# Two attention layers on one core: first f and g made in place, small PSUM reads by ScalarE, last sums by query rows

## The chip, the cores and the metric

The kernel runs on one core of one Trainium2 chip. The metric is device time in microseconds (us), the median of several executions; in each comparison the kernel before ran on the same chip in the same rounds (runs 5 to 7 on another chip than the other runs). TensorE is the matrix engine, VectorE, ScalarE and GpSimd the element-wise ones (DVE, ACT and POOL in the profile), SyncE (SP) issues most DMAs. PSUM is the memory that TensorE writes its results to; the other engines read them from there.

## The reference, cut to what matters

Eight images of 64 channels by 4096 positions pass two self-attention layers. Layer 0 has 8-channel f and g and a residual; layer 1 normalises its input by groups first.

```python
# layer 0
f, g, hh = Wf x + bf, Wg x + bg, Wh x + bh        # 8, 8 and 64 channels
beta = softmax(f^T g, axis=keys);  x = x + hh beta^T
# layer 1
xn = group_norm(x, 8 groups);  q, k, v = split(w_qkv xn + b_qkv)
x = w_proj (softmax(q k^T / 8) v) + b_proj + x
```

No maximum is subtracted ahead of the exponentials; the kernel sums them plainly and checks at the end that every sum lies in a safe range, else a general path runs.

## The kernel before

Work is cut into chunks of 1024 queries (two halves of 512) and steps of 256 keys; 16 steps make a chunk, four chunks an attention. A step is: scores on TensorE, exponentials on ScalarE into a tile `e` (six buffers), `e` against the values on TensorE, and `e` added to the running sum on VectorE. The order is layer 0 of image 0, layer 0 of image 1, then layer 1 of image 0, layer 0 of image 2, and so on. Preparing the next attention is put between the steps of the running one as "units" at given steps. Names used below: `mu` is the mean of a channel group, `v` what its deviation is made from, `a` the factor of the normalisation and `xn` the normalised input. In its parts that matter:

```python
def project(self, k):                       # Layer 0: f and g of half the columns
    ...                                     # four matmuls into one PSUM pair
    nc.scalar.activation(full, ps, AF.Identity, bias=fgb)
    nc.vector.tensor_copy(high, full)       # high: bufs=1
    nc.vector.scalar_tensor_tensor(split, high.bitcast(F32), lowmask, full, ...)
    for ...:                                # 16 small DMAs into the row tiles f, g
        self.sent = nc.sync.dma_start(dst[rows, cols], split[...])

def means():                                # Layer 1, at step 21
    ps = pair()                             # one of three PSUM pairs
    matmul(ps[:, 0, 0:1], gavg, mv[:, 0:1], start=True, stop=True)
    nc.vector.tensor_copy(mu, ps[:, 0, 0:1])
    nc.vector.tensor_sub(d, mv[:, 0:1], mu)
    nc.vector.scalar_tensor_tensor(v, d, d, mv[:, 1:2], ...)

def deviations():                           # step 24
    matmul(ps[:, 0, 0:1], gavg, v, start=True, stop=True)
    nc.vector.tensor_scalar_add(ve, ps[:, 0, 0:1], EPS)
    ...                                     # 15 VectorE operations of 128x1: a = gamma / sqrt(ve)

def normal(c):                              # step 27 for c = 0
    nc.vector.tensor_scalar(xns[c], x, mu, self.a, ...)          # xn, 128x512
                                            # step 30: TensorE projects q and k from xn

def weigh(i, j, e, cols, now):              # once a step
    ...
    added = nc.vector.tensor_add(esum, first if t == 1 else esum, e).ins   # 128x2048
```

`issue_after` puts what follows behind a named instruction of the same engine, without a wait.

## Time and profile before

| | before |
|---|---|
| time, median of 3 (range); of 4, with the result | 3088.91 us (3087.74 to 3089.83); 3088.35 |
| span of the profiled execution | 3086.4 us |
| TensorE busy | 3043.7 us |
| first dense add of VectorE | 36.10 us |
| means matmul, then copy of mu | 222.48, 231.96 us |
| xn of the first layer-1 block starts | 251.73 us |
| last exponential of the second layer-0 attention ends | 340.18 us |
| last exponential of all ends; to the end of the span | 3067.55 us; 18.9 us |

The last rows are marks along the one road.

The stretch table has the busy time of each engine within a stretch of the span, the number of its instructions, and the granted TensorE clock as a share of full speed. Of the kernel before, around the first layer-1 preparation:

```profile
core 0: us, PE busy (x) PEld busy (x) DVE busy (x) ACT busy (x) POOL busy (x), PEclk, DMA share, GB/s
...
220.00:270.00 50.00, 43.66 (x279) 15.96 (x277) 47.53 (x43) 33.73 (x29) 0.00 (x0) 0.93 0.03 6
```

TensorE misses 6.3 of these 50 us and the clock is 0.93 of full, while VectorE is busy for all but 2.5: the engine that decides this stretch is not the one with the 99%.

### The profile page before, as it was taken

Reading aid. Unit: us, or ns where it says so; the run is one execution under the profiler, and the core shown is the slowest. Engines: PE = TensorE matmul, PEld = TensorE weight load, DVE = VectorE, ACT = ScalarE, POOL = GpSimd, SP = SyncE. Lnnn points to the kernel's source line nnn. Section 1 sums busy time; section 2 is a strip of 40 time slices with the busy share of each in tenths; the row PEclk is TensorE's granted clock in tenths of the full one; section 3 lists DMA queues with packets and bytes.
Section 4 is the critical chain, followed back from the end, with each engine's and each line's share of the span. In section 5 each row is a group of like instructions: output and inputs, shape, how many; then the busy total and the mean of one; then the engine's idle time right before and its main releaser. Section 6 shows DMA issues by size and latency. Waiting matters only on the chain.

```text
span 3086.4 us, 59347 instructions
## 1 busy us (share of the span) xinstructions
PE 3043.7 (99%) x26071; PEld 1132.3 (37%) x26071; DVE 2538.6 (82%) x1616; ACT 2038.7 (66%) x1971; POOL 16.5 (1%) x41
## 2 busy tenths in 40 slices
PE   7999999999999999999999999999999999999998
PEld 2333334333343333333334333343334333334433
DVE  7999877899768997689877898779987699776676
ACT  6877655786557865578555785558855587555554
POOL 2000000000000000000000000000000000000000
PEclk9999999999999999999999999999999999999999
DMA  3000010100101001010011000100011000000000
GB/s 85 22 8 11 18 39 15 32 1 15 39 19 28 1 15 39 22 25 1 15 39 25 22 1 20 41 19 22 1 29 32 19 8 1 15 22 15 11 12 12
DMA packets 57722, 63.06 MB, mean 20 GB/s; under 512 B 30848, under 2 KB 30928, under 8 KB 57456
## 3 DMA queue, kind: packets, MB, share of 16 engines
q1 hardware_dynamic: 56336, 59.03, 7.7%
q8 instruction: 206, 3.38, 0.5%
q14 instruction: 60, 0.49, 0.1%
q0 software_dynamic: 800, 0.15, 0.0%
q10 hardware_dynamic: 320, 0.01, 0.0%
HBM read 25.06 MB, written 8.65 MB: 11 GB/s over the span
## 4 chain that ended last, share of the span: by engine, by line
PE 95%; DVE 3%; ACT 1%; issue 1%; SPq 1%; DMA 1%; ACTq 0%; DVEq 0%
PE banks L137 95%; DVE esum_l L656 2%; ACT e_l L730 0%; SPq L426 0%; ACT e_l L771 0%; DMA x<-in_x_dram 0%; DMA w<-in_WgT_dram 0%; DVE vt_l L298 0%; DVE high_l L416 0%; DVE esum_l L311 0%; SPq L145 0%; DVE r_l L355 0%; DMA fg_l<-high_l 0%; ACTq L169 0%; DVE high_l L413 0%
## 5 line engine op out<-in xcount | busy, mean ns | idle before, releaser
L656 DVE TENSOR_TENSOR esum_l<-esum_l,e_l 128x2048 f32<-128x2048 f32 x896 | 2052.3, 2291 | 455.9 <-ACT e_l L730 402.9
L730 ACT ACTIVATE e_l<-banks 128x1024 f32<-128x1024 f32 x1024 | 992.8, 1021 | 801.7 <-PE banks L137 768.8
L137 PE MATMUL banks<-e_l,v_l 64*64 64x512 f32 (+2 forms) x8772 | 1100.9, 588 | 0.0
L771 ACT ACTIVATE e_l<-banks 128x2048 f32<-128x2048 f32 (+3 forms) x763 | 955.8, 1317 | 204.2 <-PE banks L137 201.8
L137 PE MATMUL banks<-kq_l 64*64 64x512 f32 (+1 forms) x8448 | 1009.8, 586 | 6.3 <-DVE mu_l L476 6.3
L137 PE MATMUL banks<-e_l,vt_l 128*64 128x512 f32 (+1 forms) x4064 | 832.0, 550 | 0.0
L137 PEld LDWEIGHTS banks<-e_l,v_l 64*64 64x64 f32 (+1 forms) x8772 | 362.3, 133 | 574.1 <-issue 531.5
L137 PEld LDWEIGHTS banks<-kq_l 64*64 64x64 f32 (+1 forms) x8448 | 348.3, 134 | 580.2 <-issue 540.2
L137 PEld LDWEIGHTS banks<-e_l,vt_l 128*64 128x64 f32 x4064 | 267.5, 137 | 473.7 <-issue 453.7
L137 PE MATMUL banks<-fg_l 32*128 32x512 f32 x1792 | 211.0, 460 | 8.0 <-ACT e_l L771 4.4
L656 DVE TENSOR_TENSOR esum_l<-e_l,e_l 128x2048 f32<-128x2048 f32 x64 | 146.4, 2288 | 18.6 <-ACT e_l L730 9.9
L137 PEld LDWEIGHTS banks<-fg_l 32*128 32x128 f32 x1792 | 86.3, 183 | 188.5 <-ACT e_l L771 135.6
L311 DVE TENSOR_TENSOR esum_l<-esum_l 128x1024 f32<-128x1024 f32 x64 | 78.1, 1220 | 0.9
L562 DVE COPY raw_l<-banks 128x512 f32<-128x512 f32 x32 | 22.1, 691 | 31.3 <-PE banks L137 31.3
L137 PE MATMUL banks<-esum_l,ones 128*32 128x256 f32 (+1 forms) x508 | 41.3, 393 | 4.5 <-DVE esum_l L311 2.8
L360 DVE TENSOR_TENSOR raw_l<-raw_l,r_l 128x512 f32<-128x512 f32 x64 | 43.8, 684 | 0.0
L536 ACT ACTIVATE kq_l<-banks,qkb 128x512 f32<-128x512 f32 x64 | 40.6, 696 | 0.0
L137 PE MATMUL banks<-xn_l,wqk 64*64 64x512 f32 x256 | 33.4, 592 | 0.0
L137 PEld LDWEIGHTS banks<-wh,x 64*64 64x64 f32 x1024 | 22.8, 140 | 16.1 <-issue 13.9
L137 PE MATMUL banks<-x,wfg 64*64 64x512 f32 x128 | 19.2, 648 | 9.0 <-DVE low L179 9.0
L137 PEld LDWEIGHTS banks<-wvp,xn_l 64*64 64x64 f32 x1024 | 20.6, 134 | 16.9 <-issue 16.6
L445 ACT COPY raw_l<-banks 128x512 f32<-128x512 f32 x32 | 19.0, 594 | 10.9 <-PE banks L137 10.8
(88 smaller groups left out, 378.4 us busy)
## 6 DMA issues: line engine op xcount, KB each, us to landing
r_l<-recips SPq DMA_DIRECT2D x126, 128.0 KB, 2.9
fg_l<-high_l SPq DMA_DIRECT2D x224, 64.0 KB, 2.0
x<-in_x_dram SPq DMA_DIRECT2D x32, 256.0 KB, 4.8
kq_l<-kq_l SPq DMA_DIRECT2D x64, 128.0 KB, 2.3
out_dram<-raw_l SPq DMA_DIRECT2D x64, 128.0 KB, 2.3
zt_l<-zs_l SPq DMA_DIRECT2D x252, 1.0 KB, 1.7
kq_l<-high_l SPq DMA_DIRECT2D x32, 64.0 KB, 2.0
recips<-stash SPq DMA_DIRECT2D x63, 4.0 KB, 1.4
```

Of the source, the lines that this page charges most:

```text
L137: in_order(nc.tensor.matmul(*args, **kwargs))
L311: nc.vector.tensor_add(esum[:, 0], esum[:, 0], esum[:, 1])
L360: nc.vector.tensor_mul(raw, raw, r)
L445: nc.scalar.copy(raw, acc[0])
L536: nc.scalar.activation(self.parts[:, h, cols], ps[:, h, :], AF.Identity, bias=k1["qkb"][:, h : h + 1],)
L562: nc.vector.tensor_copy(raw, acc[0])
L656: added = nc.vector.tensor_add(esum, first if t == 1 else esum, e).ins
L730: nc.scalar.activation(e[:, p], both_ps[p], AF.Exp, scale=at.scale)
L771: nc.scalar.activation(e.rearrange("k p h n -> k (p h) n")[:, first_ : first_ + n_, :], banks[:, bank : bank + n_, :], AF.Exp, scale=at.scale,
```

## The change

Four intents. **Head**: f and g of the first 512 columns are made with weights laid out so that they come out in their row tiles, without DMA; the loads are reordered; the other projections and values are put between the first steps. **Constants** and **means**: small PSUM reads move from VectorE to ScalarE. **End**: the last sums are made by query rows (128x8), inverted there, and laid out over channels by a product of ones with a diagonal; the range check of all but the last sums comes earlier. Its core:

```diff
+    direct = const.tile([P, 2, P], F32, name="direct")      # weights repeated for 128 rows
...
+        def project_direct(self):
+            for i, dst in enumerate((self.f, self.g)):
+                matmul(ps[:, i, :], direct[:, i, :], x_tiles[self.b][:, 0:CW], ...)
+                nc.scalar.activation(full[:, i, :], ps[:, i, :], AF.Identity, bias=bias2[:, i : i + 1])
+                nc.vector.tensor_copy(high[:, i, :], full[:, i, :])
+                nc.vector.scalar_tensor_tensor(dst[:, 0:CW], high[:, i, :].bitcast(F32), ...)
...
+                    self.project_direct()
+                    self.project(0, (1,))                    # columns 512 to 1023, 8 DMAs
+                return [(-1, begin, True), (0, rest, True)] + [ ... values at -1, 1, 5, 8 ]
...
-                nc.vector.tensor_copy(mu, ps[:, 0, 0:1])
+                nc.scalar.copy(mu, ps[:, 0, 0:1])
...
-                nc.vector.tensor_scalar_add(ve, ps[:, 0, 0:1], EPS)
+                nc.scalar.copy(ve, ps[:, 0, 0:1])
+                nc.vector.tensor_scalar_add(ve, ve, EPS)
...
-                nc.vector.tensor_copy(wvt[:, h, :], t0[:C, 0, 0:C])     # and wvp, biases
+                nc.scalar.copy(wvt[:, h, :], t0[:C, 0, 0:C])
...
-            added = nc.vector.tensor_add(esum, first if t == 1 else esum, e).ins
+            with tc.issue_after(layers0[0].split.ins) if i == 0 and t == 1 else nullcontext():
+                added = nc.vector.tensor_add(esum, first if t == 1 else esum, e).ins
...
+        def end(self, acc, esum, e, t):
+            for part in (esum[:, 1], e[:, 0], e[:, 1]):
+                nc.vector.tensor_add(total, total, part)
+            for i, (h, k) in enumerate(parts):
+                matmul(z[:, i : i + 1], total[:, h, ts(k, P)], ones[:, 0:1], ...)
+            nc.vector.reciprocal(rt, z);  bounds(rt, 1)
+            ...                             # diag = ident * rt
+            matmul(bad_ps, ...)             # the flag
+            matmul(laid[ts(h, C), :], ones, diag[...], ...)
+            nc.vector.tensor_mul(raw, raw, laid)
```

## The prediction

> **What bounds the kernel now.** I read the page's busy shares and chain first, then the waits of TensorE, then the timeline at the three places where those waits lie.
>
> ```profile
> PE 3043.7 (99%) x26071; PEld 1132.3 (37%) x26071; DVE 2538.6 (82%) x1616; ACT 2038.7 (66%) x1971; POOL 16.5 (1%) x41
> ...
> PE 95%; DVE 3%; ACT 1%; issue 1%; SPq 1%; DMA 1%; ACTq 0%; DVEq 0%
> ```
>
> TensorE is busy 3043.7 of 3086.4 us. The change takes no large matmul away, so all that can be won is its idle time, 42.7 us, plus work done at a low clock. The list of what TensorE waited for says where that is:
>
> ```profile
> PE banks L137 <- DVE low L179: 9.0, 1, 9.0
> PE banks L137 <- DVE bad L797: 6.5, 2, 3.5
> PE banks L137 <- DVE mu_l L476: 6.3, 1, 6.3
> PE banks L137 <- ACT e_l L771: 4.4, 7, 1.9
> PE banks L137 <- DVE esum_l L311: 2.8, 1, 2.8
> PE banks L137 <- DMA fg_l<-high_l: 2.6, 2, 1.7
> ```
>
> Three places: the start (9.0, 2.6, most of the 4.4), one stall at the means of the first layer-1 block (6.3), the end (6.5 + 2.8 + 5.5 after the last matmul). The eight blocks between repeat without a wait over 1 us. The head, by the timeline:
>
> ```profile
> 8.72 0.20 DVE L174 COPY wfg<-w 128x64 f32<-128x64 f32 x1 [7.71 <-DMA w<-in_WgT_dram]
> 14.32 10.62 SPq L426 DMA_DIRECT2D fg_l<-high_l  x16
> 20.86 1.33 PE L137 MATMUL banks<-fg_l 32*128 32x512 f32 x5 [1.73 <-DMA fg_l<-high_l]
> ...
> 36.10 21.46 DVE L656 TENSOR_TENSOR esum_l<-esum_l,e_l 128x2048 f32<-128x2048 f32 x9
> ```
>
> Weights land at 8.7, the projected f and g leave by 16 small DMAs of 0.66 us each to issue, and scores run only from 20.9. At 36.1 a dense run of VectorE adds begins. Its length decides my prediction:
>
> ```profile
> 222.48 0.38 PE L137 MATMUL banks<-mv_l,gavg 128*128 128x1 f32 x2
> ...
> 231.96 0.16 DVE L476 COPY mu_l<-banks 128x1 f32<-128x1 f32 x1
> ...
> 232.17 0.79 PE L137 MATMUL banks<-kq_l 32*128 32x512 f32 x2 [6.34 <-DVE mu_l L476]
> 232.90 5.07 PE L137 MATMUL banks<-e_l,v_l 128*64 128x512 f32 x12
> ...
> 251.73 0.55 DVE L504 TENSOR_SCALAR xn_l<-x,mu_l,a_l 128x512 f32<-128x512 f32 x1
> ...
> 253.00 1.09 PE L137 MATMUL banks<-xn_l,wqk 64*64 64x512 f32 x8
> ```
>
> The means leave TensorE at 222.9, but VectorE copies them only at 231.96: it is about 9 us behind. Pairing each add with the exponential that it adds, in the trace, the add starts 1.4 us after the exponential's end at 36 us, 3.7 at 176, 8.6 at 221, and never catches up before 240. In the first two layer-0 blocks one step costs VectorE 2.39 us (2.29 and a gap of 0.1) and TensorE some 2.3, so VectorE is the slower engine from 36 to 240 us; six e buffers hide it. With the same pairing, the next write of an e buffer comes 10 us after the add that frees it at the start and only 0.5 us after it at 224. The tail:
>
> ```profile
> 3073.84 3.35 DVE L355 RECIPROCAL r_l<-banks 128x512 f32<-128x512 f32 x1
> ...
> 3078.94 1.11 SPq L570 DMA_DIRECT2D out_dram<-raw_l  x2
> ...
> 3080.71 0.14 DVE L805 CAST n_bad<-banks 1x1 int32<-1x1 f32 x1 [0.28 <-PE banks L137]
> ```
>
> **What the Trainium skill says.** "TensorE: Matmul & The Clock Gate", section on the 16 sub-arrays: VectorE and ScalarE queues are strict first-in first-out. The trace agrees: the 0.16 us copy waits 9 us behind four ready adds. Same page, "What's actually happening": after an idle window of about 3.4 us the clock halves until a busy window has passed. The trace agrees: after the 6.34 us stall twelve records took 5.07 us, and 2.37 a little later, so the stall costs some 2.7 us more. "DMA: Bandwidth & Descriptors", "Issuing engines are not separate DMA queues": transfers interleave on the same engines whoever issues them. The last 2 KB piece of the weights took 5.9 us to land while the 1 MB of x was in flight, the first 1.9; the order of issue therefore counts. "ScalarE: Activation LUTs", "What ACT_TABLE_LOAD costs": 1283 ns; here 1.28, at 8.87, behind the bias DMAs.
>
> **The change, part by part.**
>
> Head. Weights are issued first, so I put them at 3.5 us, and the first 512 columns of x at 5 (256 KB by the 2 us latency and some 170 GB/s that the first loads show). The two direct products use all 128 rows: two records of 0.85 us each at the low clock, 1.7 per product: f until 6.8, g until 8.5, and the half product for columns 512 on until 10.2. ScalarE 0.7 each, VectorE cast 0.4 and split 0.7 each (half of the 0.8 and 1.28 for 1024 wide): f and g are ready at about 11, no DMA. But the first group of scores needs a bank that the copy of the values frees, and that copy stands on VectorE behind the cast and split of the half product: ScalarE 10.3 to 11.4, cast to 12.2, split to 13.5, copy to 14.1. So scores start near 14, not 20.9: 7 us earlier for TensorE, of which the rest projection (1.7) and three groups of values (1.1 each) are put back between steps, but TensorE is not the bound here. For VectorE: the 8 DMAs of the half product take 13.5 + 5.3 to issue and 2 to land, 20.9; only then may the cast of the rest overwrite the one "high" buffer, and the diff holds the first add until the rest's split is done: 20.9 + 0.8 + 1.28 = 23.0. Three adds of 2.39 later, at 30.2, VectorE is where it was at 36.1: **5.9 us earlier**. After that it also loses two copies of wvt (0.34), wvp (0.2), two bias adds (0.3) and the mu copy (0.2): 1.0 us. **Sum 6.9.**
>
> Means by ScalarE. The bank is freed at once, so the 6.34 us stall and its 2.7 us of low clock go. But the next small matmul ("deviations", three steps or 6.8 us of TensorE work later) needs v, and two operations of v still stand in VectorE's queue 9.5 us back: TensorE waits there for about 3 us. Then projecting the normalised x (253.0) needs xn, which VectorE makes in the same queue; before, TensorE came only 0.7 us after it. So TensorE at that point cannot gain more than VectorE does: 6.9, plus the 0.7, plus some 0.5 of true VectorE idle between 225 and 252: **8.1 us for head and means together**. The stall is cut into pieces rather than removed. In the other seven blocks the means lie in a layer-1 stage where each step of 3.43 us leaves VectorE 1.14 free: nothing to win.
>
> Constants by ScalarE: the 0.5 us wait for wvt is inside the 8.1.
>
> Tail. The last full add (2.29) and the fold (1.22) become three adds of 1024, from 3066.5 to 3070.2. Then 16 records for the sums by query rows; one pair of such 128-row, one-column records took 0.38 us, so some 0.12 each: 3072.3. The reciprocal of 128x8 takes 0.2 in place of 3.35; bounds 0.7, two products for the diagonal 1.4, the two PSUM reads of the totals 1.4 (before, these lay ahead of the fold): 3076.2. The laying out by ones (0.9) lies under the totals. Multiply and residual 1.5: 3077.7, against 3078.9. The flag is no longer last (0.41 + 0.68 + 0.69 + 0.15 + the matmul and cast behind the residual go). The program's end follows each engine's last instruction by a fixed branch of some 4 us and about 1 us of closing; before, that counted from 3080.85, now from the second DMA issue on ScalarE at 3078.3: **2.6 to 3 us**.
>
> Sum: 8.1 + 2.9 = 11.0; 3088.9 - 11.0 = 3077.9.
>
> **The rivals.** (1) TensorE is not held by VectorE: it then keeps its own head gain (7 and some low-clock time, less what is put back, 4 to 8) and all of 6.3 + 2.7, and the tail: 17 to 20 us, 3069 to 3072. For it: DMA-free scores. Against it: the 0.5 us of buffer left at 224 and the unbroken adds. (2) The head is not shorter for VectorE: x lands late, or the half product's 8 DMAs and the one buffer hold the first add until 26; then only the stall's remainder and the tail count, 4 to 6 us: 3083 to 3085. (3) A wait takes the stall's place and is long enough for the clock to fall in a stage where TensorE bounds again after 253; costs 2.7 of the 11: 3081. A loss over 2% (62 us) would need a new stall in each of the eight blocks of 7 us; ScalarE has over 1 us free in every layer-1 step, so two 0.2 us copies do not make one.
>
> **Range and chances.** Centre 3077.8. One side is rival (1) in part, the other (2) or (3): 3071 to 3083. Two per cent is 62 us, more than all of TensorE's idle time, so faster 0.01, same 0.985, slower 0.005.
>
> **What would show it.** Right: in the chain, adds from about 23 us on without a gap until 240; the waits list without mu, but with one for v of 2 to 4 us and one for xn; the first dense add run 6 us earlier; the project matmul of 253.0 near 245; from there to the end of the last layer-1 step the same duration; the second output DMA near 3078 on the old clock and 5 us from there to the end. Wrong: no wait for v or xn and over 15 us gained (VectorE did not bind), a first add later than 25 us, or e exponentials waiting for adds in the blocks after 400 us.

## More of the kernel before

A scheduler in the compiler orders each engine's instructions when the kernel is built.

In the traces VectorE works through its list in the built order.

For the first layer-1 block the built VectorE list reads (running sums are "add t", t the step within the second chunk of image 1):

```
before:   add 3 | mu d v | add 4 5 6 | ve, guess | add 7 | ... | add 10 | a  xn | add 11
```

## The result, and the profile after

The changed kernel takes 3088.99 us (median of 4, 3087.75 to 3089.58), the kernel before 3088.35 in the same rounds. The ratio is 1.0001 with a 95% interval of 0.9984 to 1.0018: nothing gained. Ratios here and below are the mean time of one kernel's runs over that of the other's runs of the same rounds, so not quite the ratio of the medians. A repeat (run 11) gave 3089.46 against 3089.17.

What TensorE waited for, changed kernel (total us, times, longest):

```profile
PE banks L137 <- DMA x<-in_x_dram: 7.3, 1, 7.3
PE banks L137 <- DVE v_l L570: 4.5, 1, 4.5
...
PE banks L137 <- DVE xn_l L596: 4.0, 1, 4.0
PE banks L137 <- DVE bad L817: 2.4, 1, 2.4
...
PE banks L137 <- ACT mu_l L567: 1.2, 1, 1.2
```

Of the 6.3 us for mu 1.2 are left, now for ScalarE. In their place stand 4.5 us for v and 4.0 for xn, each once. The first product is 1.7 us earlier than before (7.3 against 9.0). The stretch of the first layer-1 preparation again:

```profile
220.00:270.00 50.00, 39.57 (x228) 13.49 (x224) 42.33 (x40) 28.45 (x29) 0.00 (x0) 0.86 0.03 6
```

TensorE is busy 4.1 us less than before in the same 50 us, at a lower mean clock (0.86 for 0.93), and VectorE, which bounded here, is now idle for 7.7 us. The timeline of that stretch (start, duration, engine, line, operation, and in brackets the idle time before it and what ended that):

```profile
222.07 0.35 PE L137 MATMUL banks<-mv_l,gavg 128*128 128x1 f32 x2 [0.59 <-DVE mv_l L561]
...
225.31 1.02 ACT L877 ACTIVATE e_l<-banks 128x1024 f32<-128x1024 f32 x1 [1.52 <-DVE esum_l L749]
226.23 0.15 ACT L567 COPY mu_l<-banks 128x1 f32<-128x1 f32 x1
...
234.90 0.22 DVE L570 SCALAR_TENSOR_TENSOR v_l<-d_l,mv_l 128x1 f32<-128x1 f32 x1
235.04 7.08 DVE L749 TENSOR_TENSOR esum_l<-esum_l,e_l 128x2048 f32<-128x2048 f32 x3
235.18 0.58 PE L137 MATMUL banks<-v_l,gavg 128*128 128x1 f32 x2 [4.51 <-DVE v_l L570]
...
255.98 0.55 DVE L596 TENSOR_SCALAR xn_l<-x,mu_l,a_l 128x512 f32<-128x512 f32 x1
256.44 2.28 DVE L749 TENSOR_TENSOR esum_l<-esum_l,e_l 128x2048 f32<-128x2048 f32 x1
256.58 1.98 PE L137 MATMUL banks<-xn_l,wqk 64*64 64x512 f32 x8 [3.97 <-DVE xn_l L596]
258.50 4.21 PE L137 MATMUL banks<-e_l,v_l 128*64 128x256 f32 x12
```

ScalarE has mu out of PSUM at 226.4, 5.7 us before VectorE had it. But v follows only at 234.9, and xn starts at 255.98, 4.25 us **later** than before, although VectorE's add of step 15 in the chunk ahead starts 1.9 us earlier than before (219.48 for 221.38). Twelve half-width records that took 2.37 us a little earlier take 4.21 at the end: the clock is down. By the clock records it is low from 234.9 to 241.8 and again from 255.4 to 262.3; before, only from 230.7 to 237.5.

The line at 225.31 shows one thing more: an exponential waits 1.5 us for an add, because all six `e` buffers are taken. ScalarE waits so four times in this trace (4.9 us in all, from 186.7 to 225.3) and never in the kernel before. So TensorE's and ScalarE's early start is stopped by VectorE's pace before the means are reached.

Why xn comes later is in the built order, which needs no chip (the traces show the same order):

```
before:   add 3 | mu d v | add 4 5 6 | ve, guess | ... | add 10 | a  xn | add 11 12 13 14
changed:  add 5 |    d v | add 6 7 8 | ve, guess | ... | add 13 | a  xn | add 14
```

The scheduler put v two adds later and xn three. An add is 2.29 us and a gap of 0.1, so three are 7.2 us. VectorE's lead at add 4 was 2.4 us (230.11 for 232.48); 7.2 - 2.4 = 4.8, close to the 4.25 that the marks show.

The head, changed kernel:

```profile
13.59 0.69 DVE L322 COPY vt_l<-banks 128x512 f32<-128x512 f32 x1 [1.34 <-PE banks L137]
...
14.20 0.74 DVE L483 SCALAR_TENSOR_TENSOR fg_l<-high_direct,lowmask,full_direct 128x512 fp32r<-128x512 f32 x1
...
14.99 0.50 PE L137 MATMUL banks<-fg_l 32*128 32x512 f32 x4 [1.46 <-DVE fg_l L483]
...
26.19 0.69 DVE L503 CAST high_l<-full_l 128x1024 fp32r<-128x1024 f32 x1 [7.92 <-DMA fg_l<-high_l]
...
28.12 2.29 DVE L749 TENSOR_TENSOR esum_l<-e_l,e_l 128x2048 f32<-128x2048 f32 x1
```

Scores start at 15.0. Before, one record of them ran at 18.3 and the others from 20.9, so the first exponential is the better mark: 16.19 for 22.20, 6.0 us earlier. The second split of the direct part, ready to run at 12.3 (its cast is done), stands behind the copy of the values and starts at 14.20; VectorE then waits 7.9 us until the eight DMAs have let go of the one `high` buffer. The fourth step's add starts at 35.30, for 36.10 before: 0.8 us won of the 5.9 that I had predicted for VectorE. Single traces differ here: the seven with this head and one `high` buffer have the fourth add at 34.2 to 35.3, the four with the old head at 36.1 to 36.7, 1.8 us apart on the average. The seven share the text of the head and still spread over 1.1 us, so marks of single traces are read here no finer than that.

The end, changed kernel:

```profile
3073.71 1.95 PE L137 MATMUL banks<-ones,esum_l 128*128 128x1 f32 x16 [0.58 <-DVE esum_l L386]
...
3078.10 0.25 PE L137 MATMUL banks<-ones,bad 128*1 128x1 f32 x4 [2.44 <-DVE bad L817]
3078.28 1.97 PE L137 MATMUL banks<-diag,ones 128*64 128x512 f32 x4
...
3080.30 0.69 DVE L415 TENSOR_TENSOR raw_end<-raw_end,banks 128x512 f32<-128x512 f32 x1 [1.48 <-PE banks L137]
```

From the last exponential's end (3070.85) to the end of the span (3087.7) it is 16.9 us, for 18.9: 2.0 us won. (The three traces with the old end have 18.9 to 19.8, the ten with this one 16.7 to 17.3: 2.4 on the average.) The laying out waits behind the flag's two small products, and runs at low clock.

The marks together: last exponential of the second layer-0 attention 340.18 before, 343.23 after (3.1 later); from there to the last exponential of all 2727.4 and 2727.6 us, so 0.25 us in all the other blocks; end 2.0 shorter. The profiled spans differ by 3.06 + 0.25 - 2.0 = 1.3 us, as 3087.7 and 3086.4 say.

### The profile page after: what moved, and what is told of

Read it like the earlier page. It is cut to its first block, busy times and chain, and to the rows that moved or that the text cites. A ratio compares the mean times of both kernels' runs of the same rounds, so it can differ in the third digit from the quotient of the medians.

```text
span 3087.7 us, 59407 instructions
## 1 busy us (share of the span) xinstructions
PE 3050.4 (99%) x26083; PEld 1133.9 (37%) x26083; DVE 2534.7 (82%) x1612; ACT 2043.5 (66%) x1999; POOL 16.5 (1%) x45
## 4 chain that ended last, share of the span: by engine, by line
PE 94%; DVE 4%; issue 1%; ACT 1%; DMA 0%; SPq 0%; DVEq 0%; ACTq 0%
PE banks L137 94%; DVE esum_l L749 3%; ACT e_l L836 0%; ACT e_l L877 0%; DVE vt_l L322 0%; DMA x<-in_x_dram 0%; DVE esum_l L386 0%; DVE esum_l L335 0%; ACT full_l L501 0%; SPq L166 0%; DVE high_l L506 0%; DVE diag L401 0%; DVE w_l L589 0%; DVE raw_l L374 0%; DVE x L540 0%
## 5 line engine op out<-in xcount | busy, mean ns | idle before, releaser
L137 PE MATMUL banks<-esum_l,ones 128*32 128x256 f32 x504 | 40.3, 391 | 1.6 <-DVE vt_l L322 1.6
L540 DVE SCALAR_TENSOR_TENSOR x<-raw_l,hb,x 128x512 f32<-128x512 f32 x32 | 24.0, 751 | 1.1
```

The source lines that it names most:

```text
L137: in_order(nc.tensor.matmul(*args, **kwargs))
L540: nc.vector.scalar_tensor_tensor(xc, o, hb, xc, op0=ALU.add, op1=ALU.add)
```

## The experiments

**Theory A** after the result: the four parts do save, but in the first layer-1 block VectorE works through its list some 9 us behind, TensorE waits there for v and xn, and what decides is how many adds stand before them in VectorE's built order. Moving the means to ScalarE made the scheduler put more adds before them. **Theory B**: the head or the ScalarE copies themselves win nothing, or cost what the others win. All runs are correct, and compared with the kernel before in the same rounds. None differs from it by 2%; only the intervals of runs 1, 5, 7, 8, 10 and 12 leave out 1.

| run | time, median (range) | before | ratio (95%) | v, xn behind add | xn starts |
|---|---|---|---|---|---|
| changed kernel | 3088.99 (3087.75 to 3089.58) | 3088.35 | 1.0001 (0.9984 to 1.0018) | 5, 13 | 255.98 |
| 1: means undone | 3082.98 (3082.32 to 3083.82) | 3088.97 | 0.9981 (0.9968 to 0.9995) | 4, 11 | 250.52 |
| 2: means only | 3091.40 (3090.31 to 3093.53) | 3088.97 | 1.0008 (0.9994 to 1.0021) | 4, 11 | 253.88 |
| 3: head only | 3088.58 (3087.51 to 3089.52) | 3088.97 | 0.9999 (0.9985 to 1.0012) | 4, 11 | 254.06 |
| 4: end only | 3087.25 (3085.35 to 3087.49) | 3088.97 | 0.9992 (0.9979 to 1.0006) | 3, 10 | 252.64 |
| 5: order pinned | 3076.24 (3075.38 to 3076.86) | 3089.52 | 0.9957 (0.9943 to 0.9970) | 2, 6 | 239.72 |
| 6: spare buffer | 3085.14 (3084.22 to 3085.68) | 3089.52 | 0.9986 (0.9973 to 1.0000) | 5, 13 | 251.51 |
| 7: 5 and 6 | 3072.52 (3072.16 to 3073.13) | 3089.52 | 0.9946 (0.9933 to 0.9960) | 2, 6 | 235.72 |
| 8: pinned, VectorE means | 3078.57 (3076.49 to 3079.86) | 3089.17 | 0.9966 (0.9952 to 0.9979) | 2, 6 | 239.29 |
| 9: as 1, xn later | 3088.11 (3086.83 to 3089.43) | 3089.17 | 0.9996 (0.9982 to 1.0009) | 4, 13 | 255.23 |
| 10: 7 and two more orders | 3068.39 (3068.10 to 3069.27) | 3089.17 | 0.9933 (0.9920 to 0.9947) | 2, 6 | 233.18 |
| 11: changed kernel again | 3089.46 (3087.92 to 3089.59) | 3089.17 | 0.9999 (0.9985 to 1.0013) | 5, 13 | 256.00 |
| 12: pinned, no head | 3078.22 (3077.59 to 3078.52) | 3089.16 | 0.9964 (0.9952 to 0.9977) | 1, 5 | 239.49 |

### 1. The means undone

```diff
-                nc.scalar.copy(mu, ps[:, 0, 0:1])
+                nc.vector.tensor_copy(mu, ps[:, 0, 0:1])
...                                        # and ve likewise, as before
```

> The whole change with one part undone: the two means leave PSUM by VectorE again. Theory A (VectorE's queue order decides): in the built program xn of the first layer-1 block stands behind add 11 of its chunk, not behind add 13 as in the changed kernel and not behind add 10 as before. One add is 2.39 us, head start of VectorE 1.9 us: xn at about 252, 4 us earlier than in the changed kernel; the single stall at mu is back (5 to 7 us), the waits for v and xn are gone, one low-clock period in place of two. Time 3085 to 3087.5, some 2 to 4 us under the changed kernel. Theory B (the two ScalarE copies are harmless and the loss lies in the head): 3088 to 3089.5, as the changed kernel.

Measured 3082.98, 6.0 us under the kernel before. The waits for v and xn are gone, the stall at mu (5.6 us) is back, one low-clock period (229.3 to 236.1) is left, and xn starts at 250.52. So the other three parts are worth 6 us, and the means take them all back. It beat my range (3085 to 3087.5): I had not counted what the constants do, see run 3. That this is all of the difference is not shown; the first add of this trace is also 1.0 us earlier (27.08 for 28.12) with the same head.

### 2. The means alone

The same four lines, put into the kernel before.

> The kernel before with only the two means copies moved to ScalarE. Theory A: the mu stall of 6.3 us turns into waits for v and xn; xn stands behind add 11 instead of 10, so it comes 2.2 us later; time 3088.5 to 3092, not faster than before. Theory B (a stall removed is time won): 6.3 us and some 2.7 us of low clock go, 3079 to 3082.

Measured 3091.40, 2.4 us over the kernel before by the medians (the interval of the ratio includes 1). Theory B's 6.3 and 2.7 us are not there: TensorE waits 5.0 us for v and 3.1 for xn, and xn is 2.15 us later than before, one add. Taking the stall's reason away moved the stall.

### 3. The head alone

The new loads, the direct projection, the units between the steps, and the hold on the first add; all else as before.

> The kernel before with only the head of the change (direct f and g, order of loads, projection and values put between steps). Theory A: VectorE's first dense add comes only some 1 to 2 us earlier than before (27 to 28 us is the first add, one high buffer), xn stands one add later (11, not 10): time 3087 to 3090, nothing won although scores start 6 us earlier. Theory B (scores start earlier, so the head alone wins 5 to 8 us): 3080 to 3083.

Measured 3088.58: nothing. The scores' start is as early as in the whole change. But with the constants still on VectorE, a new wait comes up:

```profile
68.39 0.34 DVE L270 COPY wvt<-banks 64x64 f32<-64x64 f32 x2
...
68.78 0.69 PE L137 MATMUL banks<-wp,wvt 64*128 64x64 f32 x2 [4.70 <-DVE wvt L270]
```

TensorE waits 4.7 us for two copies of 0.34 us together, behind VectorE's adds, and the clock is low from 65.8 to 72.6. In the kernel before the same wait is 0.5 us, since VectorE is less far behind there (an add near 58 us starts 5.6 us after its exponential with the head alone, 1.6 before). By the add of step 15 ahead of the means the head alone stands at 221.85, the kernel with head, constants and end (run 1) at 218.44. So the constants on ScalarE are worth some 3 us with the head (3.4, of which 0.4 stand already at the fourth add); this is a difference of two runs, not a run of its own.

### 4. The end alone

> The kernel before with only the new end. Both theories: the end of the last exponential to the end of the program falls from 18.9 to about 16.9 us, so 3086 to 3087; the rest of the trace unchanged.

Measured 3087.25, 1.7 under the kernel before (the interval includes 1). From the last exponential (3068.47) to the end of the span (3085.785) it is 17.3 us, 1.5 less than before, for the 2.0 expected.

### 5. The order pinned

```diff
+        def hold(self, made):              # first layer-1 block only
+            nonlocal held
+            if self.b == 0:
+                held = made.ins
...                                        # called with v, with a, and with the first xn
-            with tc.issue_after(layers0[0].split.ins) if i == 0 and t == 1 else nullcontext():
+            ahead = layers0[0].split.ins if i == 0 and t == 1 else held
+            with tc.issue_after(ahead) if ahead is not None else nullcontext():
                 added = nc.vector.tensor_add(esum, first if t == 1 else esum, e).ins
```

> The changed kernel, same instructions, only VectorE's order pinned for the first layer-1 block: adds traced after the means, the deviations and the first normalising are issued behind them, so v stands behind add 2 (not 5) and xn behind add 6 (not 13). Theory A: no wait for v or xn over 1 us, no low-clock period near 235 or 255; VectorE's 12 us of waiting for exponentials between 225 and 345 mostly goes; last exponential of the second layer-0 block near 331 instead of 343; time 3075 to 3079. Theory B (loss elsewhere): 3087 to 3090.

Measured 3076.24, within the range, 13.3 us under the kernel before. Not one instruction was added or taken away; only VectorE's order differs. The stretch, and the timeline in it:

```profile
220.00:270.00 50.00, 47.66 (x308) 17.05 (x308) 48.37 (x42) 39.78 (x40) 0.00 (x0) 1.00 0.05 12
```

```profile
227.34 0.22 DVE L577 SCALAR_TENSOR_TENSOR v_l<-d_l,mv_l 128x1 f32<-128x1 f32 x1
...
230.22 0.38 PE L137 MATMUL banks<-v_l,gavg 128*128 128x1 f32 x2
...
239.72 0.54 DVE L603 TENSOR_SCALAR xn_l<-x,mu_l,a_l 128x512 f32<-128x512 f32 x1
...
245.24 1.39 PE L137 MATMUL banks<-xn_l,wqk 64*64 64x512 f32 x8
```

Neither product has a wait in brackets: v is there 2.7 us ahead of TensorE, xn 5.0. VectorE is busy 48.4 of 50 us, the clock full throughout. The last exponential of the second layer-0 attention ends at 330.23, 13.0 us earlier than in the changed kernel: all of the gain is made here. The adds are then up to 11.5 us behind the exponentials, more than before, and the six `e` buffers do run out: ScalarE waits eight times for an add, 6.5 us in all. But TensorE's waits for exponentials are 4.3 us, as in the changed kernel (4.4), and each layer-1 step then leaves VectorE 1.14 us free to catch up. So the exchange paid.

### 6. A spare buffer

```diff
-            high = work.tile([P, 2, CW], F32R, tag="high", bufs=1, name=f"high_{n}")
+            if len(js) == 1:
+                high = ppool.tile([P, 2, CW], F32R, tag="e", name=f"high_{n}")   # an e buffer is lent
+            else:
+                high = work.tile([P, 2, CW], F32R, tag="high", bufs=1, name=f"high_{n}")
```

(Two buffers outright did not fit, and a kernel with the chain from mu to xn on GpSimd, away from VectorE's list, did not compile. Neither was run.)

> The changed kernel with a second buffer for the half projection's high part (an e buffer is lent), so the rest's cast need not wait for its 8 DMAs; order as in the changed kernel (v behind add 5, xn behind 13). Theory A (first add held by the one buffer): first add at 21 to 23 instead of 28.1, v and xn some 4 to 6 us earlier, waits for them cut to under 3 us together with fewer low-clock periods; time 3081 to 3085. Theory B (the buffer is not what holds the first add): 3087 to 3090.

Measured 3085.14, just over the range. The first add starts at 21.22, for 28.12, so the one buffer is what held it; xn is 4.5 us earlier, and the time 4.4 us lower than before. But I had expected the two waits to shrink to under 3 us together. They are 4.4 and 5.4. TensorE reaches the means earlier too (their input mv is made at 217.21, for 221.67), so the distance between the engines, which is what the waits are made of, stays. A head start moves such a wait forward; it doesn't remove it.

### 7. Both

> Both: order pinned and the spare buffer. Theory A: the two add up only in part, since with the order pinned TensorE already runs nearly without a gap from 28 us on; time 3072 to 3077. Theory B: 3087 to 3090.

Measured 3072.52: another 3.7 us under run 5, less than the 7.3 by which the first add is earlier (20.42 for 27.76), but near the 4.2 by which the fourth is (30.74 for 34.94).

### 8. The order pinned, means on VectorE

Runs 1 and 5 together.

> The changed kernel with VectorE's order pinned as in the pinned run, but the two means leave PSUM by VectorE as in the kernel before; mu stands behind add 2. It tells what the ScalarE copies are worth once the order is right. If the order is all: TensorE waits 2 to 4 us for mu (one low-clock period at most), and the time is 3076 to 3080, within 4 us of the pinned run. If the ScalarE copies are the real gain: the stall of 5 to 6 us stays and the time is 3081 to 3084, as with the means undone and the order free.

Measured 3078.57. Two of its five executions lie in the range of run 5, three are 1.7 to 3.0 us above it, on another chip; the intervals of the ratios overlap. The wait for mu is 0.8 us, less than I had expected. So with the order right, who reads the means makes no difference that these runs can tell; one of 2 to 3 us in favour of ScalarE is not ruled out.

### 9. The dose the other way

The kernel of run 1 has no ScalarE copy of the means. One edge is added that puts its xn behind add 13:

```diff
+        if i == NC + 1 and t == 13 and first_normal:
+            tc.add_manual_dep(first_normal[0], added.name, <issue order only>, reason="later")
```

> The dose the other way: the kernel with the means undone (3083.0), no ScalarE copy, one edge added that puts xn behind add 13 in place of add 11, and nothing else moved. Theory A: xn two adds of 2.39 us later, at about 255.3; TensorE waits 3 to 4 us for it; with a low-clock period of some 3 us behind it the time is 3086.5 to 3090, so the loss comes back without any ScalarE copy. Theory B (the ScalarE copies themselves cost): 3082 to 3084, unchanged.

Measured 3088.11, for 3082.98: the loss is back, with the means on VectorE.

```profile
255.23 0.54 DVE L597 TENSOR_SCALAR xn_l<-x,mu_l,a_l 128x512 f32<-128x512 f32 x1
...
255.83 1.09 PE L137 MATMUL banks<-xn_l,wqk 64*64 64x512 f32 x8 [3.43 <-DVE xn_l L597]
```

xn is 4.7 us later than in run 1 (two adds), TensorE waits 3.4 us, and the clock falls for a second time, from 257.0 to 260.4. No execution of this run comes within 3 us of the slowest of run 1, on the same chip. (The low period at mu is also longer here, 10.2 us for 6.8, but TensorE reaches the product of v only 0.2 us later than in run 1, so the rest comes behind it.) For the copies of the means theory B is out: the position of one half-microsecond instruction is enough.

### 10. Two more orders

In run 7, the second direct split is put ahead of the copy of the values, and the flag's products behind the laying out:

```diff
+            with tc.issue_after(self.direct_split) if first_ else nullcontext():
                 copy(self.vt[:, :, ts(c, TPC), :], ...)
...
-            matmul(bad_ps, ...); nc.vector.tensor_copy(n_bad, bad_ps)
             matmul(laid[ts(h, C), :], ones, diag[...], ...)
+            matmul(bad_ps, ...); nc.vector.tensor_copy(n_bad, bad_ps)
```

> The pinned order and the spare buffer, and two more orders mended: the second direct split ahead of the copy of the values (it stood behind it and started 1.9 us late), and the flag's two small matmuls behind the laying out by ones (it waited 2.4 us for them). Theory A: first scores 1 to 2 us earlier, the last multiply 0.5 to 1.5 us earlier; time 3069.5 to 3072. If the head is not on the path any more: 3071.5 to 3072.5 from the tail alone.

Measured 3068.39, lower than expected and the best here: 20.8 us under the kernel before, ratio 0.9933. Scores start at 14.33. The clock records show no low period near the start, where all the other runs have one of 7 to 14 us between 15 and 31 us; that was not intended, and I did not test how much of the 4.1 us against run 7 (measured on another chip) it makes.

```profile
12.72 0.75 DVE L484 SCALAR_TENSOR_TENSOR fg_l<-high_direct,lowmask,full_direct 128x512 fp32r<-128x512 f32 x1
...
13.59 0.69 DVE L323 COPY vt_l<-banks 128x512 f32<-128x512 f32 x1
```

The split starts 1.5 us earlier than in the changed kernel, on a first product that is 0.5 us later (TensorE's wait for x is 7.7 us here). From the last exponential (3051.25) to the end of the span (3067.14) it is 15.9 us, 1.0 less than in the changed kernel.

### 11. The changed kernel again

> The changed kernel itself, on the same chip as the runs beside it: 3088 to 3090, within 1.5 us of the kernel before; waits for v (4.5) and xn (4.0) and two low-clock periods between 230 and 265 us as in its first trace.

As expected in time and marks (first add 28.15, xn 256.00); the wait for v is 4.5 us again, the one for xn 5.5 for the 4.0 expected. The first of the two low-clock periods was 3.4 us long here (235.1 to 238.5) and 6.8 in the first trace, after the same wait of 4.5 us.

### 12. The order pinned, without the head

> The pinned kernel without the new head: means, constants and end as in the change, VectorE's order pinned (v behind add 1, xn behind add 5), loads and first projections as in the kernel before. It tells what the head is worth once nothing behind it takes its gain back. In the first traces the 16th exponential of the first chunk ends 5.3 us earlier with the new head (56.8 against 62.1), VectorE's dense run only 0.8. If the head's gain is TensorE's: 5 us over the pinned run, 3080 to 3082.5. If VectorE's pace bounds: 1 to 2 us over it, 3077 to 3078.5.

Measured 3078.22, a ratio of 0.9964 for the pinned kernel's 0.9957: the head is worth about 2 us, as VectorE's pace has it, though scores start 6 us earlier with it. The intervals overlap and the order is not quite the same (behind adds 1 and 5 here, 2 and 6 there), so the 2 us are a rough size; a gain of 5 to 6 us does not fit.

## Why the prediction was wrong

**The means: the mechanism was right, one assumed fact was not.** The prediction said that the stall would be "cut into pieces rather than removed", by a wait for v of about 3 us and by xn, and both came (4.5 and 4.0). It then bounded TensorE at xn by VectorE's own gain, 8.1 us. The step that failed is "xn, which VectorE makes in the same queue": it took for granted that xn stands where it stood before, behind add 10. The built order had it behind add 13, 7.2 us of adds more. Run 9 shows that such a shift alone brings the loss, run 5 that taking it away (and more) brings some 13 us, more than the 11 predicted in all. Why the scheduler places the chain later when ScalarE makes the copies is not settled; the listings show only that it does, in both kernels (10 to 11 in the kernel before, 11 to 13 in the changed one). The slack in the `e` buffers was taken as unchanged too: the prediction had 0.5 us between an add and the next write of its buffer at 224 us; in the changed kernel, by the same pairing, it is 0.1 us from 219 to 225, and exponentials wait. What that alone cost was not measured.

**The head: the term for VectorE was mis-sized.** Predicted 5.9, measured 0.8 at the fourth add (1.8 over all traces). The first columns of x landed at 7.2, not 5. The second split stood behind the copy of the values (1.9 us), and the half projection could not write its `full` tile until that split was done. The eight DMAs therefore left from 18.3, not 13.5, and the rest's split ended at 28.2, not 23.0. The prediction's own sign of being wrong, "a first add later than 25 us", was there, at 28.1, and with it rival (2), whose bound was 26. The step after it was right: the one buffer and the hold on the first add do set when the dense run begins (run 6), and TensorE's early scores alone win nothing (run 3). The second term, 1.0 us for the constants, missed that with the head they also keep TensorE from a 4.7 us wait.

**The low clock** was rival (3) and came true: a second period, from 255.4 to 262.3, partly in a stretch where TensorE bounds again. I had given it 2.7 us, and that was its size for this period: the two groups of records from 256.58 on took 1.98 and 4.21 us, where such groups take 1.09 and 2.37 at full clock, 2.7 more. The centre left it out.

**The end**: 2.0 us for 2.9 (2.4 over all traces). The laying out was counted at 0.9 us under other work; it took 1.97, at low clock, behind the flag's products, for which TensorE waited 2.4 us.

**The other blocks**: right. Between the marks at 340 and 3067 us the time differs by 0.25 us.

Put together, the prediction's 8.1 us for head and means became a loss of 3.1, and the end's 2.9 became 2.0. The range (3071 to 3083) held no case in which the parts cancel: each rival kept the VectorE order of the kernel before, and the 3083 to 3085 of rival (2) lay outside it. (A small slip: by the terms of rival (1), 4 to 8, 9.0 and 2.9, its low end is 16 us, not 17.) That the time stays within 2% was right, and says little at this size.

## What to carry to other kernels

Three things that these runs show. Where an engine runs behind, a short instruction costs what stands before it in that engine's list, not its own length; after moving an operation to another engine, look at the built order of the engine that it left, and pin the few instructions on which the bounding engine waits ahead of those that have buffers to spare. A stall that is removed shows its worth only at the next place where the same two engines meet, so follow marks along the road and not the list of stalls. And an early start of one engine is worth no more than the early start of the engine that bounds the stretch behind it.

## What the Trainium skill lacked or had wrong

- "TensorE: Matmul & The Clock Gate", the section on the 16 sub-arrays, says that VectorE and ScalarE take their instructions strictly in order. No page says what follows for a kernel whose order a scheduler sets at build time: the same instructions in another VectorE order took 3088.99 and 3076.24 us (the kernel before beside them 3088.35 and 3089.52), and one instruction two adds further back cost 5.1 us (runs 1 and 9).
- The same page's "What's actually happening" gives windows of about 3.4 us. The runs agree: low periods ahead of the program's end last 3.4, 6.8, 10.2 or 13.7 us, multiples of 3.41, and the same wait of 4.5 us was followed by 6.8 us in one trace and 3.4 in another. Its table has the half clock after at least one idle window. Here the window need not be idle throughout: in the changed kernel the clock fell at 16.5 us, and in the 3.4 us before that TensorE was busy for 1.25 us and its longest wait was 1.46. Further down the page tells of short idles that do this, without a figure.
- "Advanced Engine Details and Errata", "Control Flow Timing", puts a compare-and-branch at about 108 ns. The branch that skips the general path at the end is in the trace of the kernel before as 3.81 us on TensorE; on ScalarE and VectorE the next instruction comes 3.6 us after it, on GpSimd and SyncE 0.4 to 0.5. The program's last 5.5 us are mostly this. "Runtime: NRT & Kernel Launch", "Instruction fetch mechanics", does say that a taken branch out of the fetched pages waits for a fetch, but has no figure; whether this is such a case is not shown.
- "Runtime: NRT & Kernel Launch", the preamble breakdown, has register loads from device memory (about 1.3 us for several), none from on-chip memory. Loading the flag from on-chip memory into a register took 0.47 to 0.54 us on the five engines before, and 1.18 on ScalarE directly behind its DMA issue in the changed kernel.
